# Graph layer with sorted edges: narrower chunks of edges and another interleaving in the token loop

## The chip, the cores and the metric

One NeuronCore of a Trainium2 chip runs the whole program. The time is the device time of one execution in microseconds (us). A profile records one execution, instruction by instruction. Engines: TensorE (PE, with its weight loads as PEld), VectorE (DVE), ScalarE (ACT), GpSimd (POOL) and SyncE (SP), which here mostly issues DMA transfers.

## The reference

The layer takes 1250 tokens (graph nodes) of 768 numbers and 20,000 edges, sorted by their destination. It adds a graph attention block (two attention layers) and a linear attention block to x, and then a mixture of experts:

```python
src = jax.random.randint(..., (20000,), 0, 1250); dst = jax.random.randint(..., (20000,), 0, 1250)
_o = jnp.argsort(dst, stable=True); src = src[_o]; dst = dst[_o]
def gat_conv(x, src, dst, W, a_src, a_dst, bias, H, C, n):
    h = (x @ W).reshape(n, H, C)
    ...
    e = leaky_relu(s_src[src] + s_dst[dst]); emax = segment_max(e, dst)
    ee = exp(e - emax[dst]); alpha = ee / segment_sum(ee, dst)[dst]
    return segment_sum(alpha * h[src], dst) + bias
xn = _layernorm(x)
x = x + gnn(xn, edges) + linear_attention(xn)
x = x + experts(_layernorm(x))
```

The edges go through both attention layers only as sums over (source, destination) pairs, so it is enough to know how many edges each pair has.

## The kernel before

The tokens are ten tiles of 125 rows. The attention works on a dense table cntT of edge counts: 125 partitions (the low part lo of the source) by ten source tiles by 1250 destinations, plus the table absent that marks pairs without an edge. The function gps_block has these stages: set-up of weights (until about 55 us), the token loop (59 to 210 us), keys and values, queries, the two attention layers, the router, and from about 940 us the blocks of the experts. The change is in the set-up and the token loop.

**Counting.** The 20,000 sorted edges are 160 chunks (ECH) of 125 edges, one edge per partition. An edge has a key = destination x 10 + source tile, and rel = key - base, where base belongs to its chunk: ten times the first destination that the chunk is taken to reach. For each chunk, DVE compares the steps 0, 1, 2, ... with rel (line 377, tile wide, 500 columns of 16 bit, 1 where the edge's key is). For eight chunks at a time, DVE compares the steps with lo (line 374, tile los). PE multiplies the two (line 387): the product adds the chunk's edges to counts in PSUM (pc), 125 by 500 for a block of 50 destinations (CB). A chunk reaches at most two blocks, so it gives one or two products, each only over its columns. There are six buffers of wide, whose second half is zeros, written once by POOL (line 345); the zeros are read where a product opens a block and has to write all of its 500 columns.

When the last chunk of a block is in, the function counted has ACT copy the counts to cntT (line 348). When a tile of 125 destinations is complete, the function there adds the loops of nodes on themselves (DVE, line 356), has ACT copy the tile to 16 bits (358), PE transpose it in two groups of five (ptc, 362) and DVE compare each group with zero (absent, 363).

**Edges outside.** The kernel takes sorted edges to lie near their expected place: chunk c reaches from destination (c // 16) x 125 + (c % 16) x 8 - 22 over CW = 50 destinations. Lines 328 to 336 count the edges outside of this (off, offs, a product po, off_i). After the token loop all engines read off_i (line 424), and where it isn't zero, a branch (425) counts everything again with full masks.

**Token loop.** For each tile, DVE normalises (401), POOL adds the bias (402), PE transposes in two groups of three (pt, 406), ACT copies to xnT (407), and PE makes two times six products with the graph weights (ph, 411, 400 columns in 32 bit), whose sums DVE scales into G (415). The chunks are a generator, parts, from which the loop takes one chunk after an even product k and two after an odd one (nine for six products).

**Order.** A planner places each instruction on its engine's queue with estimated times and priorities, so an engine's order is near that of the code and not the same; each engine then works its queue in order. 11 of the 120 token products are placed behind the branch.

Of the kernel before, what the change touches and what calls it, by code (L numbers as in the profile page):

```python
# [1 line left out]

# [6 lines left out]
F32 = mybir.dt.float32  # L9
F16 = mybir.dt.float16  # L10
# [5 lines left out]
ALU = mybir.AluOpType  # L16
# [3 lines left out]
P = 128  # L20
TP = 125
NT = 10
N = TP * NT
# [10 lines left out]
NPAIR = NH // 2  # L34
NE, HID, HS = 8, 768, 384
ECH = 160
CB, CW = 50, 50
HT = NT

# [9 lines left out]
CG = CO + 2  # L51

TINY = 2.0 ** -64


def part_bcast(ap, parts, n):
# [5 lines left out]
def gps_block(ctx: ExitStack, tc: tile.TileContext, x, src, dst, norm_g, norm_b, W1, a_src1, a_dst1, b1,  # L62
              W2, a_src2, a_dst2, b2, Wu, bu, w_qkv, w_proj, b_proj, router_w, w_gate, w_up, w_down,
              ws_gate, ws_up, ws_down, sg_w, sg_b, out):
    nc = tc.nc
# [33 lines left out]
    edp = edpool.enter_context(tc.tile_pool(name="edges", bufs=1, side="right", reuse_waits="tile"))  # L99
    wg = edp.tile([P, KD, H1 * CG], F32, name="wg")  # L100

    steps16 = edp.tile([TP, 2 * CB * HT], F16, name="steps16")
    nc.gpsimd.iota(steps16, pattern=[[1, 2 * CB * HT]], base=0, channel_multiplier=0,
                   allow_small_or_imprecise_dtypes=True)
# [6 lines left out]
    lo16 = edp.tile([TP, ECH], F16, name="lo16")  # L111
    key = edp.tile([TP, ECH], F32, name="key")
    rel = edp.tile([TP, ECH], F32, name="rel")
    bw = edp.tile([TP, 2, 2 * CG], F32, name="bw")
    bias = edp.tile([TP, 2, HALF], F32, name="bias")

# [44 lines left out]
    with tc.tile_pool(name="ph1", bufs=1, reuse_waits="tile") as p1, tc.tile_pool(name="ph1w", bufs=2, reuse_waits="tile") as p1w, \  # L161
# [55 lines left out]
        for j in range(2):  # L217
            o = H2 * (C2 + 1) + j * H2
# [11 lines left out]
        for k in range(KD):  # L230
# [10 lines left out]
            for h in range(H1):  # L241
                o = (h % 2) * CG
                for i in range(2):
                    nc.tensor.matmul(pm[:, h // 2, o:o + CG], wt[:, 2 * h + i, :], w2x[:, 2 * h + i, :],
                                     start=(i == 0), stop=(i == 1))
# [5 lines left out]
        for h in range(H1):  # L251
            o = (h % 2) * CG
# [9 lines left out]
        for s in range(2):  # L262
            half = slice(s * HALF, (s + 1) * HALF)
            nc.tensor.matmul(pb2[:, s, :HALF], ones[:2, :], br[:, half], start=True, stop=False)
            for h in range(H2):
                nc.tensor.matmul(pb2[:, s, :HALF], bc[:, 24 + h:25 + h].to_broadcast([C2, TP]), wub[:, h, half], start=False,
                                 stop=(h == H2 - 1))
# [5 lines left out]
        for h in range(H2):  # L273
            o = h * (C2 + 1) + C2
# [16 lines left out]
        nc.vector.tensor_scalar(hi, src_f, float(TP), None, op0=ALU.is_ge)  # L291
        for m in range(2, HT):
            nc.vector.scalar_tensor_tensor(hi, src_f, float(m * TP), hi, op0=ALU.is_ge, op1=ALU.add)
        nc.vector.scalar_tensor_tensor(lo, hi, -float(TP), src_f, op0=ALU.mult, op1=ALU.add)
        nc.vector.tensor_copy(lo16, lo)
        nc.vector.scalar_tensor_tensor(key, dst_f, float(HT), hi, op0=ALU.mult, op1=ALU.add)

        base = p1.tile([TP, ECH], F32, name="base")
        nc.gpsimd.iota(base, pattern=[[TP * HT, ECH // 16], [8 * HT, 16]], base=-22 * HT, channel_multiplier=0,
                       allow_small_or_imprecise_dtypes=True)  # L300
        nc.vector.tensor_sub(rel, key, base)

    def weights(dst_tile, w):
# [14 lines left out]
    with tc.tile_pool(name="cnt", bufs=1, reuse_waits="tile") as cp, \  # L318
# [7 lines left out]

        off = cp.tile([TP, ECH], F32, name="off")
        nc.vector.tensor_scalar(off, rel, 0.0, None, op0=ALU.is_lt)
        nc.vector.scalar_tensor_tensor(off, rel, float(CW * HT), off, op0=ALU.is_ge, op1=ALU.add)
        offs = cp.tile([TP, 2], F32, name="offs")  # L330
        nc.vector.tensor_reduce(offs[:, 0:1], off, axis=AX.X, op=ALU.add)
        nc.vector.memset(offs[:, 1:2], 1.0)
        po = ps.tile([P, 4, P], F32, name="po", tag="tr")
        nc.tensor.matmul(po[0:1, 0, 0:1], offs[:, 0:1], offs[:, 1:2], start=True, stop=True)
        off_i = cp.tile([1, 1], I32, name="off_i")
        nc.vector.tensor_copy(off_i, po[0:1, 0, 0:1])

        NB = N // CB
        BC = CB * HT
        firsts = [c // 16 * TP + c % 16 * 8 - 22 for c in range(ECH)]  # L340
        reach = [range(max(f, 0) // CB, (min(f + CW, N) - 1) // CB + 1) for f in firsts]

        wide = [cp.tile([TP, 2 * BC], F16, name=f"wide{i}") for i in range(6)]
        for w in wide:
            nc.gpsimd.memset(w[:, BC:], 0.0)

# [21 lines left out]
        def chunks():  # L368
            LB = 8
            open_ = {}  # L370
            for c in range(ECH):
                if c % LB == 0:
                    los = cp.tile([TP, LB, TP], F16, name="los", bufs=2)
                    nc.vector.tensor_tensor(los, lo16[:, c:c + LB, None].to_broadcast([TP, LB, TP]),
                                            steps16[:, None, :TP].to_broadcast([TP, LB, TP]), ALU.is_equal)
                w = wide[c % 6]
                nc.vector.tensor_scalar(w[:, :BC], steps16[:, :BC], rel[:, c:c + 1], None, op0=ALU.is_equal)
                for b in reach[c]:
                    new = b not in open_
                    if new:  # L380
                        open_[b] = pcp.tile([TP, 512], F32, name="pc")

                    o = (b * CB - firsts[c]) * HT
                    a = max(-o, 0)
                    e = BC if new else min(BC, BC - o)
                    last = c == ECH - 1 or b not in reach[c + 1]
                    nc.tensor.matmul(open_[b][:, a:e], los[:, c % LB, :], w[:, o + a:o + e], start=new, stop=last)
                    if last:
                        counted(b, open_.pop(b))
                yield  # L390

        parts = chunks()
        for t0 in range(0, NT, 2):
            ts = range(t0, t0 + 2)
            mv, r, r2 = ahead
            if t0 + 2 < NT:
                ahead = norm(t0 + 2)
            for i, t in enumerate(ts):
                tok = slice(t * TP, (t + 1) * TP)
                xn = p1w_.tile([TP, D], F32, name="xn")  # L400
                nc.vector.tensor_scalar(xn, acc[:, t, :], mv[:, i, 0:1], r[:, i:i + 1], op0=ALU.subtract, op1=ALU.mult)
                nc.gpsimd.tensor_add(acc[:, t, :], acc[:, t, :], bias.rearrange("p s d -> p (s d)"))
                for k0 in range(0, KD, 3):
                    pt = ps.tile([P, 4, P], F32, name="pt", tag="tr")
                    for k in range(3):
                        nc.tensor.transpose(pt[:, k, :TP], xn[:, (k0 + k) * P:(k0 + k + 1) * P], ident[:TP, :TP])
                    nc.scalar.copy(xnT[:, k0:k0 + 3, tok], pt[:, 0:3, :TP])
                for s in range(2):
                    ph = ps.tile([TP, 512], F32, name="ph", tag="mm", bufs=3)
                    for k in range(KD):  # L410
                        nc.tensor.matmul(ph[:, :2 * CG], xnT[:, k, tok], wg[:, k, s * 2 * CG:(s + 1) * 2 * CG],  # L411
                                         start=(k == 0), stop=(k == KD - 1))
                        for _ in range(1 + k % 2):
                            next(parts, None)
                    nc.vector.scalar_tensor_tensor(G[:, t, 2 * s:2 * s + 2].rearrange("p h c -> p (h c)"),
                                                   ph[:, :2 * CG], r2[:, i:i + 1], bw[:, s], op0=ALU.mult, op1=ALU.add)
                nc.gpsimd.tensor_copy(s1[:, t].rearrange("p j h -> p h j"), G[:, t, :, CO:CG])
                nc.gpsimd.memset(G[:, t, :, CO:CO + 1], 1.0)
# [6 lines left out]
        with tc.If(n_off > 0):  # L425
            for b0 in range(0, NB, 2):
# [3 lines left out]
                for c in range(ECH):  # L430
                    nc.vector.tensor_scalar(lof[c % 2], steps16[:, :TP], lo[:, c:c + 1], None, op0=ALU.is_equal)
                    nc.vector.tensor_scalar(wide[c % 2], steps16, relg[:, c:c + 1], None, op0=ALU.is_equal)
                    for i, pc in enumerate(pcs):
                        nc.tensor.matmul(pc[:, :BC], lof[c % 2], wide[c % 2][:, i * BC:(i + 1) * BC],
                                         start=(c == 0), stop=(c == ECH - 1))
# [26 lines left out]
    class Largest:  # L462


        def __init__(self, name, ss, sd, H):
            self.name, self.ss, self.sd, self.H = name, ss, sd, H
            self.srow = rows(ss, H, f"{name}_srow", TINY)
            self.mx = p3.tile([TP, NT, H], F32, name=f"{name}_mx")
# [15 lines left out]
        def columns(self):  # L484

            name, H, ss, sd = self.name, self.H, self.ss, self.sd
            z = p3.tile([TP, NT, H], F32, name=f"{name}_z")
            nc.vector.scalar_tensor_tensor(z, self.mx, 1.0 / TINY, sd, op0=ALU.mult, op1=ALU.add)
            em = p3.tile([TP, NT, H], F32, name=f"{name}_em")
# [9 lines left out]
    with tc.tile_pool(name="ph2", bufs=1, reuse_waits="tile") as p2:  # L499
# [14 lines left out]
        with tc.tile_pool(name="kvw", bufs=2, side="right", reuse_waits="tile") as p2w, tc.tile_pool(name="kvps", bufs=2, space=PSUM, reuse_waits="tile") as ps:  # L514
# [5 lines left out]
            for pr in range(0, NPAIR, 2):  # L520

                wkv = wkv0
                if pr > 0:
                    wkv = (p2w if pr == 2 else early).tile([P, KD, 2, 2 * P], F32, name=f"wkv{pr}", bufs=1,
                                                           tag="wkv" if pr == 2 else "early")
# [81 lines left out]
    with tc.tile_pool(name="h2p", bufs=1, reuse_waits="tile") as hp, tc.tile_pool(name="gatw", bufs=2, reuse_waits="tile") as pw:  # L607
# [87 lines left out]
        with tc.tile_pool(name="wup", bufs=1, side="right", reuse_waits="tile") as wp2, \  # L695
# [55 lines left out]
            o = H2 * (C2 + 1)  # L751
# [54 lines left out]
    with tc.tile_pool(name="fln", bufs=2, reuse_waits="tile") as pw, tc.tile_pool(name="flnps", bufs=2, space=PSUM, reuse_waits="tile") as ps:  # L806
# [4 lines left out]
                                base=0, pattern=[[1, TP]], channel_multiplier=-1)  # L811
        steps = pw.tile([TP, NE, -(-N // PART)], F32, name="steps", bufs=1)
        nc.gpsimd.iota(steps, pattern=[[0, NE], [PART, -(-N // PART)]], base=0, channel_multiplier=0,
                       allow_small_or_imprecise_dtypes=True)
        jb = pw.tile([TP, NBLK * NPART, NE], F32, name="jb", bufs=1)
        nc.gpsimd.iota(jb, pattern=[[1, NBLK * NPART], [0, NE]], base=0, channel_multiplier=0,
                       allow_small_or_imprecise_dtypes=True)
        odd = pw.tile([TP, -(-NBLK // 2), 2], F32, name="odd", bufs=1)
        nc.gpsimd.iota(odd, pattern=[[0, -(-NBLK // 2)], [1, 2]], base=0, channel_multiplier=0,
                       allow_small_or_imprecise_dtypes=True)  # L820
# [4 lines left out]
                       allow_small_or_imprecise_dtypes=True)  # L825
        rev = pw.tile([TP, NT, NE], F32, name="rev", bufs=1)
        nc.gpsimd.iota(rev, pattern=[[0, NT], [-1, NE]], base=NE, channel_multiplier=0,
                       allow_small_or_imprecise_dtypes=True)
# [18 lines left out]
        for r in range(2):  # L847
            m = pw.tile([TP, NT], F32, name=f"r_m{r}", bufs=1)
            nc.vector.tensor_reduce(m, pb, axis=AX.X, op=ALU.max)
            o = pw.tile(S3, F32, name=f"r_o{r}", bufs=1)  # L850
            nc.vector.tensor_tensor(o, pb, m[:, :, None].to_broadcast(S3), ALU.is_equal)
            nc.vector.tensor_mul(o, o, rev)
            f = pw.tile([TP, NT], F32, name=f"r_f{r}", bufs=1)
# [10 lines left out]
        pc = ps.tile([P, 512], F32, name="pc", tag="m")[:TP, :2 * NT * NE].rearrange("p (i t e) -> p i t e", i=2, e=NE)  # L864
# [14 lines left out]
        for e in range(NE):  # L879
# [3 lines left out]
                                       op0=ALU.mult, op1=ALU.add)  # L883
# [16 lines left out]
        for r in range(2):  # L900
# [7 lines left out]
            for t in range(NT):  # L908
                nc.tensor.matmul(pids[:, r * NBLK:(r + 1) * NBLK], spot[:, t, :], numb[:, t, :], start=(t == 0),
                                 stop=(t == NT - 1))  # L910
# [38 lines left out]
        for c0, cw in CHUNKS:  # L949
            for f in range(nh):  # L950
                pg = sps.tile([P, 512], F32, name="pg")
                pu = sps.tile([P, 512], F32, name="pu3")
                for pt, i in ((pg, 0), (pu, 1)):
                    for k in range(KD):
                        nc.tensor.matmul(pt[:, :cw], wsg[i][:, k, f * P:(f + 1) * P], xnT[:, k, c0:c0 + cw],
                                         start=(k == 0), stop=(k == KD - 1))
# [152 lines left out]
    with tc.tile_pool(name="comb", bufs=1, reuse_waits="tile") as cb, tc.tile_pool(name="cps", bufs=3, space=PSUM, reuse_waits="tile") as ps:  # L1109
# [12 lines left out]
        for t in range(2, NT):  # L1122
# [6 lines left out]
            for u in range(2 * (t - 3), min(2 * (t - 3) + 2, NT)):  # L1129
                for r in range(2):  # L1130
                    nc.vector.scalar_tensor_tensor(acc[:, u, :], ygs[u][:TP, r, :], g2[:, u, r:r + 1], acc[:, u, :],  # L1131
                                                   op0=ALU.mult, op1=ALU.add)
# [31 lines left out]
```

## Time and profile before

| | |
|---|---|
| median of 3 runs | 1597.15 us (1594.57 to 1598.87) |
| the profiled execution | 1597.16 us, span 1595.1 us |
| PE busy | 1525.0 us, 96% |
| DVE busy | 724.4 us, 45% |
| ACT busy | 367.6 us, 23% |
| POOL busy | 98.1 us, 6% |
| first and last chunk product | 59.6 and 190.9 us |

The span is from the first to the last instruction in the profile. Busy shares are averages over stages; in the token loop DVE is far busier than its 45%. A row of instructions gives line, engine, operation, output <- input, shapes and count, then the busy time in us and the mean duration of one in ns, then the engine's idle time right before these instructions and who ended it. A row of waits gives who waited for whom, the total in us, the number of waits and the longest. Durations of PE products include the time until the results are out, during which the next product already runs; the time from start to start is shorter.

### The profile page before, as it was taken

How to read it: one execution, taken by the hardware profiler on the slowest of the kernel's cores; microseconds unless marked ns; L12 is line 12 of the kernel's file. 1: busy time of each engine (PE TensorE's matmuls, PEld its weight loads, DVE VectorE, ACT ScalarE, POOL GpSimd, SP SyncE). 2: the span in 40 equal slices, each digit the busy share in tenths (PEclk: the TensorE clock that was granted, in tenths of full speed). 3: DMA queues.
4: the chain of work that ended last, by engine and by line, in shares of the span. 5: the costliest groups of instructions: out<-in, count | busy, mean ns of one | idle time of the engine just before them, and what ended most of it. 6: DMA issues, size and time to landing. Idle time of an engine off the chain costs nothing. (4 is left out here: it accounts for less than half of the span.)

```text
span 1595.1 us, 18670 instructions
## 1 busy us (share of the span) xinstructions
PE 1525.0 (96%) x7143; PEld 855.7 (54%) x7143; DVE 724.4 (45%) x1355; ACT 367.6 (23%) x630; POOL 98.1 (6%) x144
## 2 busy tenths in 40 slices
PE   5999889999999989999999999999999999999986
PEld 5666544444454669896555554444444444444443
DVE  7889639411535359996799651111111111111116
ACT  3222211111101048881276310101111010111100
POOL 2211000000000000000000100000100001000000
PEclk9999989999999999999999999999999999999998
DMA  7100031001201111002121343688888888888727
GB/s 202 40 1 1 2 132 65 7 0 50 63 10 50 40 46 33 33 17 78 33 62 49 108 176 151 218 316 321 301 311 317 317 308 307 307 326 312 265 101 270
DMA packets 92835, 229.18 MB, mean 144 GB/s; under 512 B 5431, under 2 KB 28061, under 8 KB 92742
## 3 DMA queue, kind: packets, MB, share of 16 engines
q1 hardware_dynamic: 84428, 199.30, 35.8%
q0 software_dynamic: 6112, 27.95, 5.0%
q8 instruction: 64, 1.05, 0.3%
q10 hardware_dynamic: 2202, 0.64, 0.2%
q14 instruction: 29, 0.24, 0.0%
HBM read 212.42 MB, written 16.43 MB: 143 GB/s over the span
## 5 line engine op out<-in xcount | busy, mean ns | idle before, releaser
L1012 PE MATMUL pgb<-wg,xT 128*64 128x384 f32 (+1 forms) x1056 | 178.8, 488 | 0.5 <-ACT xT L1019 0.5
L1012 PE MATMUL pdb<-wd,hT 128*64 128x384 f32 (+1 forms) x1056 | 175.1, 488 | 1.4 <-SPq L1092 1.4
L1012 PE MATMUL pub<-wu,xT 128*64 128x384 f32 (+1 forms) x1056 | 174.0, 486 | 0.0
L533 PE MATMUL pp<-wkv,xnT 128*125 128x512 f32 x360 | 160.8, 595 | 0.1
L615 PE MATMUL pa<-G,u 125*125 125x199 f32 x800 | 140.4, 336 | 11.2 <-DVE h L623 6.0
L615 PEld LDWEIGHTS pa<-G,u 125*125 125x125 f32 x800 | 135.6, 189 | 16.2 <-issue 7.2
L1012 PEld LDWEIGHTS pub<-wu,xT 128*64 128x64 f32 x1056 | 75.7, 137 | 94.5 <-issue 94.5
L1012 PEld LDWEIGHTS pdb<-wd,hT 128*64 128x64 f32 x1056 | 74.6, 137 | 91.6 <-issue 87.0
L1012 PEld LDWEIGHTS pgb<-wg,xT 128*64 128x64 f32 x1056 | 73.7, 137 | 90.7 <-issue 89.8
L533 PEld LDWEIGHTS pp<-wkv,xnT 128*125 128x125 f32 x360 | 65.6, 189 | 73.1 <-issue 72.7
L1031 DVE TENSOR_TENSOR h<-h,pgb 128x384 f32<-128x384 f32 x44 | 24.4, 554 | 171.7 <-ACT h L1030 171.7
L1042 DVE COPY y<-pdb 128x768 f32<-128x768 f32 x22 | 21.1, 958 | 178.8 <-PE pdb L1012 178.8
L411 PE MATMUL ph<-wg,xnT 128*125 128x400 f32 x240 | 99.6, 521 | 2.5 <-PEq L425 2.4
L598 DVE SCALAR_TENSOR_TENSOR u<-ea,cntT 125x625 f32<-125x625 f32 x120 | 93.9, 805 | 12.6 <-PE pa L615 8.0
L595 ACT ACTIVATE eb<-r,g_ss 125x625 f32<-125x625 f32 x120 | 95.0, 816 | 20.3 <-DVE ea L596 20.3
L596 DVE TENSOR_TENSOR ea<-ea,eb 125x625 f32<-125x625 f32 x120 | 94.0, 805 | 8.2 <-ACT ea L593 5.4
L480 DVE CUSTOM_DVE_ANT_0 junk<-ssb,absent 125x1250 bf16<-125x1250 f32 x60 | 87.8, 1463 | 11.7 <-DMA ssb<-g_srow_d 10.4
L1030 ACT ACTIVATE h<-pgb 128x384 f32<-128x384 f32 x44 | 21.6, 491 | 307.6 <-PE pgb L1012 307.6
L563 PE MATMUL pq<-xnT,wq 128*128 128x500 f32 (+1 forms) x216 | 82.6, 527 | 4.6 <-DMA wq<-in_L_mix_w_qkv_dram 4.5
L1036 DVE TENSOR_TENSOR h<-h,pub 128x384 f32<-128x384 f32 x44 | 24.4, 554 | 134.4 <-PE pub L1012 134.4
L715 PE MATMUL pu<-wu,xnT 128*125 128x384 f32 x240 | 82.1, 487 | 1.3 <-DVE acc L720 1.3
L576 PE MATMUL pu<-wp,at 128*125 128x384 f32 x240 | 80.4, 488 | 1.0 <-DVE acc L579 1.0
(267 smaller groups left out, 1666.9 us busy)
## 6 DMA issues: line engine op xcount, KB each, us to landing
wg<-in_L_ffn_w_gate_dram SPq DMA_DIRECT2D x22, 2304.0 KB, 8.4
wu<-in_L_ffn_w_up_dram SPq DMA_DIRECT2D x22, 2304.0 KB, 10.4
wd<-in_L_ffn_w_down_dram SPq DMA_DIRECT2D x22, 2304.0 KB, 9.6
yg<-ys SPq DMA_DIRECT2D x10, 768.0 KB, 9.4
r<-g_rrow_d SPq DMA_DIRECT2D x12, 625.0 KB, 4.0
wq<-in_L_mix_w_qkv_dram SPq DMA_DIRECT2D x18, 384.0 KB, 3.5
wkv<-in_L_mix_w_qkv_dram SPq DMA_DIRECT2D x6, 768.0 KB, 12.3
acc<-in_x_dram POOLq DMA_DIRECT2D x10, 375.0 KB, 10.6
```

The costliest lines, as they stand in the source:

```text
L411: nc.tensor.matmul(ph[:, :2 * CG], xnT[:, k, tok], wg[:, k, s * 2 * CG:(s + 1) * 2 * CG], start=(k == 0), stop=(k == KD - 1))
L480: nc.vector.tensor_tensor_reduce(out=junk, in0=self.ssb[:TP], in1=absent[:, dt, :], scale=1.0, scalar=-3.0e38, op0=ALU.add, op1=ALU.max, a ...
L533: nc.tensor.matmul(pp, xnT[:, k, tok], wkv[:, k, :, :], start=(k == 0), stop=(k == KD - 1))
L563: nc.tensor.matmul(pq[:, :qw], wq[:, k, :], xnT[:, k, tok], start=(k == 0), stop=(k == KD - 1))
L576: nc.tensor.matmul(pu[:, s, :HALF], at[:, k, i * TP:(i + 1) * TP], wp[:, k, s * HALF:(s + 1) * HALF], start=(k == 0), stop=(k == KD - 1))
L595: nc.scalar.activation(eb, r[:TP, 1, :], AF.Exp, bias=ss02[:, st, h:h + 1])
L596: nc.vector.tensor_max(ea, ea, eb)
L598: nc.vector.scalar_tensor_tensor(u, ea, 1.0, cntT[:, st, half * W:(half + 1) * W], op0=ALU.min, op1=ALU.mult)
L615: nc.tensor.matmul(pa[i][:, :CO + 1], u[:, i * TP:(i + 1) * TP], G[:, st, h, :CO + 1], start=(st == 0), stop=(st == NT - 1))
L715: nc.tensor.matmul(pu[:, :HALF], xnT[:, k, t * TP:(t + 1) * TP], wus[s][:, k, :], start=(k == 0), stop=(k == KD - 1))
L1012: nc.tensor.matmul(pt[part, :HALF], rows[:, k, part], w[:, k, s * HALF:(s + 1) * HALF], start=(k == 0), stop=(k == KD - 1))
L1031: nc.vector.tensor_mul(h, h, pgs[s][:, :HALF])
```

## The change

The reach of a chunk follows its place. The 160 chunks are 20 spans (SPANS) of eight (SPAN). Sorted random destinations stray most in the middle and little at the ends, so each span has its own margin STRAY (9 nodes at the ends to 20 in the middle) and WIDTH = 2 x STRAY + 9 (27 to 49 nodes). The function first_of gives a chunk's first destination. A mask is then WIDTH x 10 columns wide (270 to 490) where no block is opened, else 500 as before.

base is now filled span by span, with a new tile reached that holds the width (20 iotas and 20 memsets on POOL in place of one iota). The check for edges outside compares with reached (one DVE instruction more), its product goes to the PSUM pool of the counts, and off_i is copied by ACT. wide has eight buffers. In the token loop four chunks are taken after product 2 and five after product 5 of each six.

```diff
-CB, CW = 50, 50
+CB = 50
+SPAN = 8
+SPANS = ECH // SPAN
+STRAY = [math.ceil(40 * ((n := min(g + 1, SPANS - g)) * (SPANS - n)) ** 0.5 / SPANS) for g in range(SPANS)]
+WIDTH = [2 * m + 9 for m in STRAY]
...
+def first_of(c):
+    g, i = divmod(c, SPAN)
+    return g * N // SPANS + i * 8 - STRAY[g]
...
+    reached = edp.tile([TP, ECH], F32, name="reached")
...
-        nc.gpsimd.iota(base, pattern=[[TP * HT, ECH // 16], [8 * HT, 16]], base=-22 * HT, channel_multiplier=0,
-                       allow_small_or_imprecise_dtypes=True)
+        for g in range(SPANS):
+            cols = slice(g * SPAN, (g + 1) * SPAN)
+            nc.gpsimd.iota(base[:, cols], pattern=[[8 * HT, SPAN]], base=first_of(g * SPAN) * HT, channel_multiplier=0,
+                           allow_small_or_imprecise_dtypes=True)
+            nc.gpsimd.memset(reached[:, cols], float(WIDTH[g] * HT))
...
-        nc.vector.scalar_tensor_tensor(off, rel, float(CW * HT), off, op0=ALU.is_ge, op1=ALU.add)
+        far = cp.tile([TP, ECH], F32, name="far")
+        nc.vector.tensor_tensor(far, rel, reached, ALU.is_ge)
+        nc.vector.tensor_add(off, off, far)
...
-        po = ps.tile([P, 4, P], F32, name="po", tag="tr")
-        nc.tensor.matmul(po[0:1, 0, 0:1], offs[:, 0:1], offs[:, 1:2], start=True, stop=True)
+        po = pcp.tile([TP, 512], F32, name="pc")
+        nc.tensor.matmul(po[0:1, 0:1], offs[:, 0:1], offs[:, 1:2], start=True, stop=True)
         off_i = cp.tile([1, 1], I32, name="off_i")
-        nc.vector.tensor_copy(off_i, po[0:1, 0, 0:1])
+        nc.scalar.copy(off_i, po[0:1, 0:1])
...
-        firsts = [c // 16 * TP + c % 16 * 8 - 22 for c in range(ECH)]
-        reach = [range(max(f, 0) // CB, (min(f + CW, N) - 1) // CB + 1) for f in firsts]
-        wide = [cp.tile([TP, 2 * BC], F16, name=f"wide{i}") for i in range(6)]
+        firsts = [first_of(c) for c in range(ECH)]
+        cols = [WIDTH[c // SPAN] * HT for c in range(ECH)]
+        reach = [range(max(f, 0) // CB, (min(f + w // HT, N) - 1) // CB + 1) for f, w in zip(firsts, cols)]
+        wide = [cp.tile([TP, 2 * BC], F16, name=f"wide{i}") for i in range(8)]
...
-                w = wide[c % 6]
-                nc.vector.tensor_scalar(w[:, :BC], steps16[:, :BC], rel[:, c:c + 1], None, op0=ALU.is_equal)
+                w = wide[c % len(wide)]
+                n = cols[c] if all(b in open_ for b in reach[c]) else BC
+                nc.vector.tensor_scalar(w[:, :n], steps16[:, :n], rel[:, c:c + 1], None, op0=ALU.is_equal)
...
-                    e = BC if new else min(BC, BC - o)
+                    e = BC if new else min(BC, cols[c] - o)
...
-                        for _ in range(1 + k % 2):
+                        for _ in range({2: 4, 5: 5}.get(k, 0)):
                             next(parts, None)
```

## The prediction

> **What bounds the kernel now.** I read the busy digits first, then the same engines over the stretch that the change touches, then what waited there, then single instructions. The page:
>
> ```profile
> PE   5999889999999989999999999999999999999986
> DVE  7889639411535359996799651111111111111116
> ACT  3222211111101048881276310101111010111100
> PEclk9999989999999999999999999999999999999998
> ```
>
> One digit is 39.9 us. TensorE (PE) is at 9 nearly everywhere. The token loop lies in digits 2 to 5; there VectorE (DVE) shows 8 too, so the stage needs both engines looked at. Busy time by stretch (clock third from the right; the counts in brackets are instructions):
>
> ```profile
> 60.00:194.90 134.90, 129.02 (x677) 82.70 (x676) 110.53 (x278) 35.57 (x60) 18.29 (x26) 1.00 0.01 3
> 194.90:205.10 10.20, 7.77 (x15) 3.86 (x16) 0.57 (x1) 0.95 (x2) 0.00 (x0) 0.50 0.02 5
> ```
>
> In 134.9 us PE is busy for 129.0 (96%), DVE for 110.5 (82%). Then come 10.2 us at half clock. The waits of this stretch:
>
> ```profile
> ACT cntT L348 <- PE pc L387: 76.2, 22, 5.3
> DVE wide L377 <- PE pc L387: 12.2, 24, 1.0
> PE ptc L362 <- ACT c L358: 4.2, 4, 1.6
> PE ph L411 <- PEq L425: 2.4, 1, 2.4
> PE pt L406 <- DVE absent L363: 1.4, 4, 0.6
> ```
>
> DVE waits 12.2 us for PE to hand back mask buffers; PE waits for no mask at all. PE sets the pace, interrupted by short chains through ScalarE (ACT) and DVE. What one product costs:
>
> ```profile
> L387 PE MATMUL pc<-wide,los 125*125 125x500 f16 x30 | 11.3, 376 | 0.0
> L387 PE MATMUL pc<-wide,los 125*125 125x100 f16 x10 | 2.1, 206 | 0.0
> L411 PE MATMUL ph<-wg,xnT 128*125 128x400 f32 x240 | 99.6, 521 | 2.5 <-PEq L425 2.4
> L377 DVE TENSOR_SCALAR wide<-steps,rel 125x500 f16<-125x500 f16 x160 | 50.7, 355 | 12.6 <-PE pc L387 12.2
> ```
>
> A mean contains the pipeline's latency, which the next product overlaps; the price is the slope: (376 - 206) / 400 columns = 0.425 ns a column. A token product (120 in the code, 240 passes in the row) takes 2 x 335 ns from start to start in the trace. A mask of 500 columns takes 258 ns start to start on DVE.
>
> **The change, part by part.**
>
> *Fewer columns.* Counting the chunk products as the built programs list them: 309 with 90,370 columns before, 291 with 79,530 after. 10,840 x 0.425 ns = 4.6 us off PE. The stage has no slack on PE, so this is gained in full unless something else becomes late.
>
> *Fewer changes between the two kinds of product.* Ahead of the branch the built order has 109 token products in 85 stretches before, in 33 after. From start to start, the 83 stretches of two or more passes have a first pass that takes 1.9 us in all beyond 335 ns each, and the chunk products right before a stretch 1.5 us in all beyond their columns: 3.4 us, 40 ns a stretch. 52 x 40 ns = 2.1 us; between 0.5 (were only the median of some 10 ns real) and 2.1. I take 2.0, as the mean is what adds up.
>
> *The chain chunk, count, transposes.* Each of ten transposed tiles (ptc) needs the last product of its counts, an ACT copy (0.58), a DVE addition (0.29), an ACT copy (1.24): 2.1 us. In the built order before, PE has 2.0 to 2.3 us of other work in between nine times and 0.7 us the last time; after, 2.1 to 2.8 nine times and none the last. That costs 0.7 us at the end of the stage. The 5-wide transposes pt that follow a ptc need its PSUM buffers back, two DVE instructions (absent) of 0.76 us. Before, two such places have little work between (0.84 and 0.63 us of chunk products), and the trace shows 0.5 and 0.9 us lost there. After, four have: 0.54, 0.64, 1.16 and 0.65 us of work, so by the same rows about 0.6, 0.9, 0.2 and 0.8 us. Loss 1.0 us. Last places of the stage:
>
> ```profile
> 193.41 0.79 PE L362 MATMUL ptc<-ident,c 125*125 125x125 f16 x10 [1.59 <-ACT c L358]
> 194.81 1.60 PE L406 MATMUL pt<-ident,xn 125*128 125x125 f32 x6 [0.61 <-DVE absent L363]
> 200.36 9.98 PE L411 MATMUL ph<-wg,xnT 128*125 128x400 f32 x22 [2.43 <-PEq L425]
> ```
>
> *Half clock there.* The Trainium skill ("TensorE: Matmul & The Clock Gate", "Part 1: The HAM clock gate") says that idling over a window of about 3.4 us halves the clock, and that windows run freely. The row: 194.9 to 205.1 at 0.50, three such windows, just after the idle places above, and none from 60 to 194.9. By the row alone the tail stays as it is, cost 0; by the rule the phase can shift it by a window either way, and 3.4 us at half clock costs 1.7 us. I take 0 and keep 1.7 both ways.
>
> *VectorE.* Mask columns fall from 80,000 to 70,250. 258 ns for 500 columns is, with four elements a cycle at 0.96 GHz (an estimate by the first page below), 0.26 ns a column over a fixed 128; 9,750 x 0.26 = 2.5 us off DVE, hidden behind PE, gain 0. Here a rule speaks against the change: widths are (2m + 9) x 10, so half of 490 is 245, an odd number of 2-byte elements. "VectorE: DVE Perf Modes", section "Mode 2×_1P — pack two bf16 into one 32-bit read", asks for 4-byte alignment; "Vector Engine (DVE) Microarchitecture Reference", section "5.1 Performance modes — why throughput varies by op and dtype", measured that it makes no difference if the count is even. The row L377 has only 500, whose half is even. By the first, 57,750 columns in 135 masks cost 0.52 instead of 0.26 ns: DVE up 12.5 us against before; by the second, down 2.5. I take the second, as it is a measurement of this shape, and keep the first as a rival. Group by group, with DVE at most eight chunks ahead, DVE falls behind once, by 0.8 us (chunks 31 to 42, where PE has no token product); a ptc wait lies there anyway. Cost 0, at most 0.8.
>
> *The check for stray edges.* One DVE instruction more (0.24 us, L329's kind, start to start) ahead of the first chunk. In it, off_i moves to ACT: DVE loses a wait of 3.32 us on the product po, and ACT gets a copy of some 0.2 us (as short as its 125x2 ones) between b1w and the xnT copies; PE has four chunk products (0.55 us) before it needs xnT. PE is busy until 59.1 us with L271, so nothing of this shows; without that cover it would be 0.2 to 0.5 us. po's place in another PSUM pool frees a transpose buffer: nothing waits for it.
>
> *GpSimd (POOL).* One iota becomes 20 iotas and 20 memsets, plus two memsets of 0.51 us for the new mask buffers:
>
> ```profile
> 23.70 0.32 POOL L299 IOTA base<- 125x160 f32 x1
> 32.41 0.73 POOL L322 MEMSET rest<- 3x768 f32 x1 [8.38 <-PE p_w L235]
> 40.45 0.97 POOL L345 MEMSET wide<- 125x500 f16 x2 [6.39 <-DVE bw L239]
> ```
>
> 40 instructions at 0.16 (L418's memset) to 0.32 us are 6.4 to 12.8 us, ending at 30 to 36.5. Queued behind are rest, whose store SP issues at 33.2 and which would be up to 4 us late, and the mask memsets, which idle 6.4 us until 40.45 anyway. SP's next load behind it waits until 54.65 for other work. rel needs base at 51.3. Cost 0; were POOL four times slower, 51.3 would be missed.
>
> Sum: -4.6 - 2.0 + 0.7 + 1.0 = -4.9 us. What follows the loop keeps its length and starts earlier. The profiled execution took 1597.16 us (span 1595.1, 2.1 around it), the median of the runs is 1597.15: the sum needs no scaling. **1592.2 us.**
>
> **The rivals.**
>
> *B, more than the sum:* a mask lead of eight chunks in place of six gets the DVE addition out earlier, and the three ptc waits of about 0.9 us beyond the usual 0.2 vanish (2.2 us), and a half-clock window goes at the end (1.7): 1588.3. For it: DVE did wait 12.2 us for buffers. Against it: two additions stand right behind a 1.19 us los instruction in the new order too.
>
> *C, the gain is given back on PE:* idle time at ptc and pt now falls together. The trace has 1.2 us of idling around 105 us without loss of clock and 1.6 us at the end with it; three of the four new places have up to 1.9 us. Two windows at half clock cost 3.4: 1595.6.
>
> *D, slower, VectorE becomes the bound:* half-rate masks. DVE's 110.5 us become 123.0; its own waits on others (24.4 idle less the 12.2 for buffers) add 12.2: 135.2, as long as the 134.9 of before. Half of the 9 us that PE waits fall outside of it, and 0.7 at the end: +5.3, 1602.5. It decides once a mask of 490 columns takes about 0.36 us start to start; at 0.26 it is gone. Against it: the measured page.
>
> *E, the change doesn't do what it says:* an edge outside its chunk's reach would send the kernel through the branch that counts all again. The reference's edges stay five nodes inside the low end and nine inside the high end of every chunk's reach. Excluded.
>
> **How the numbers follow.** As summed 0.54: its centre lies at the bound of 0.3% (4.8 us, about what a measurement of this kernel can tell), spread 2 us, leaning to the faster side by the switches that could hide more: 0.33 faster, 0.21 within. B 0.17, faster. C 0.09, within. D 0.20, slower. Faster 0.50, same 0.30, slower 0.20. The likeliest case alone spans 1589 to 1595. The range: half of D is above 1602.5, and a twentieth to a tenth, B's far end, below 1586.5.
>
> **What would show it.** Column slope unchanged and 291 chunk products: the 4.6. The last chunk product at about 185 instead of 190.9 us. Mask rows of 490 columns near 355 ns mean (A) or near 480 (D); a PE wait on DVE's masks, absent now, would mean D. Digits below 10 in the clock between 60 and 185 us: C. POOL's last reached later than 51 us, or DVE idle before rel, would undo the POOL step. It goes wrong if the waits at ptc grow from their 4.2 us by more than 2.

## The result, and the profile after

| | before | after |
|---|---|---|
| median | 1596.26 us (1594.47 to 1598.87, 7 runs) | 1590.88 us (1585.89 to 1593.91, 7 runs) |
| ratio, 95% interval | | 0.9956 [0.9939, 0.9974] |
| the profiled execution | 1597.16 us, span 1595.1 | 1587.15 us, span 1585.4 |
| mean granted clock of PE | 0.985 | 0.992 |
| first and last chunk product | 59.62 and 190.87 us | 56.58 and 184.73 us |
| next stage (keys and values) starts | 211.07 us | 204.02 us |

The kernel became faster by 0.44% [0.26, 0.61], 7.0 us by that ratio and 5.4 us between the medians of all runs. The profiled pair differs by 10.0 us, more than either, and its page has to be read with that in mind: 3.0 us lie ahead of the first chunk product, 4.0 us between it and the next stage (151.45 against 147.44), and some 2.6 us behind that, in stages that the change leaves alone.

The busy digits of the profile after:

```profile
PE   5999889998999989999999999999999999999996
DVE  7888559311726359896799551111111111111116
ACT  3222211111101058881376310101111010111100
PEclk9999999999999999999999999999999999999998
```

PE is as full as before. Its busy time by stretch, with the clock third from the right, first the token loop up to its last chunk, then the end of the stage:

```profile
60.00:187.00 127.00, 120.10 (x633) 78.08 (x632) 100.53 (x270) 34.52 (x58) 17.80 (x26) 1.00 0.00 1
187.00:200.00 13.00, 8.38 (x31) 4.75 (x32) 2.16 (x3) 1.11 (x3) 0.00 (x0) 0.87 0.02 5
```

PE works 95% of the loop and DVE 79%, so PE still sets the pace. The clock is full throughout the loop. At the end it is halved for 3.4 us here; a second profile of the same kernel (a0_after below) has 10.2 us of it, as before had. The waits in the loop:

```profile
ACT cntT L369 <- PE pc L409: 68.9, 21, 5.9
PE ptc L383 <- ACT c L379: 5.6, 4, 2.3
DVE wide L399 <- PE pc L409: 5.1, 7, 1.6
PE ph L433 <- PEq L448: 3.6, 1, 3.6
PE pt L428 <- DVE absent L384: 1.6, 7, 0.6
PE pc L409 <- DVE wide L399: 0.6, 1, 0.6
```

DVE waits 5.1 us for mask buffers in place of 12.2. PE waits at ptc for 5.6 us (4.2 before), at pt for 1.6 (1.4), and now once for a mask, 0.6. The groups, with busy time and mean ns of one:

```profile
L433 PE MATMUL ph<-wg,xnT 128*125 128x400 f32 x240 | 89.0, 511 | 3.7 <-PEq L448 3.6
L409 PE MATMUL pc<-wide,los 125*125 125x500 f16 x25 | 9.4, 376 | 0.0
L409 PE MATMUL pc<-wide,los 125*125 125x270 f16 x12 | 3.0, 278 | 0.0
L399 DVE TENSOR_SCALAR wide<-steps,rel 125x490 f16<-125x490 f16 x54 | 16.4, 344 | 0.9 <-PE pc L409 0.9
```

A column still costs (376 - 278) / 230 = 0.426 ns. A mask of 490 columns has a mean of 344 ns, no more than one of 500 had (355). Last, the end of the stage in order of time:

```profile
187.22 0.79 PE L383 MATMUL ptc<-ident,c 125*125 125x125 f16 x10 [2.26 <-ACT c L379]
...
188.62 0.54 PE L428 MATMUL pt<-ident,xn 125*128 125x125 f32 x3 [0.61 <-DVE absent L384]
...
194.27 9.02 PE L433 MATMUL ph<-wg,xnT 128*125 128x400 f32 x22 [3.61 <-PEq L448]
```

The last count tile makes PE wait 2.26 us, 0.67 more than the 1.59 of before.

These rows agree with what the prediction said of a column, of a mask and of the last wait. Two things they leave open. The 4.0 us between the first chunk product and the next stage are less than the 4.9 forecast for the loop, although this end of the stage has less half clock; in a0_after, with the same 10.2 us of it as before, that stretch takes 148.83 us, 2.6 less than the 151.45 of before. And the prediction doesn't explain the 3.0 us ahead of the first chunk product.

### The profile page after: what moved, and what is told of

The parts are those of the page before. It is cut to its first block, busy times and chain, and to the rows that moved or that the text cites. A ratio compares the mean times of both kernels' runs of the same rounds, so it can differ in the third digit from the quotient of the medians.

```text
span 1585.4 us, 18641 instructions
## 1 busy us (share of the span) xinstructions
PE 1512.6 (95%) x7125; PEld 849.4 (54%) x7125; DVE 720.0 (45%) x1355; ACT 367.6 (23%) x631; POOL 99.0 (6%) x185
## 5 line engine op out<-in xcount | busy, mean ns | idle before, releaser
L503 DVE CUSTOM_DVE_ANT_0 junk<-ssb,absent 125x1250 bf16<-125x1250 f32 x60 | 87.8, 1463 | 12.2 <-DMA ssb<-g_srow_d 10.9
L433 PE MATMUL ph<-wg,xnT 128*125 128x400 f32 x240 | 89.0, 511 | 3.7 <-PEq L448 3.6
```

The source lines that it names most:

```text
L503: nc.vector.tensor_tensor_reduce(out=junk, in0=self.ssb[:TP], in1=absent[:, dt, :], scale=1.0, scalar=-3.0e38, op0=ALU.add, op1=ALU.max, a ...
```

## The experiments

Ratios are against runs of the kernel before on the same chip, beside those of the experiment; a gain or loss in us below is the ratio times the median of before. "First pc" is the first chunk product, "next stage" the first product pp of the keys and values, both of the profiled execution.

| | median us | ratio | first pc | next stage |
|---|---|---|---|---|
| n0_before | 1596.82 | 1.0000 [0.9992, 1.0009] | 56.6 | 211.0 |
| e1_reach | 1591.70 | 0.9968 [0.9956, 0.9979] | 55.8 | 206.4 |
| e2_interleave | 1597.89 | 1.0002 [0.9993, 1.0011] | 55.6 | 214.0 |
| e3_six | 1591.38 | 0.9968 [0.9955, 0.9980] | 56.9 | 206.1 |
| a0_after | 1590.97 | 0.9965 [0.9951, 0.9978] | 55.7 | 204.5 |
| e4_old_po | 1593.28 | 0.9977 [0.9967, 0.9987] | 54.8 | 208.1 |
| e5_full_masks | 1590.40 | 0.9958 [0.9945, 0.9971] | 56.4 | 206.6 |
| e6_ten | 1591.80 | 0.9968 [0.9956, 0.9980] | 60.3 | 205.3 |
| e7_po_only | 1591.89 | 0.9979 [0.9971, 0.9987] | 55.8 | 206.3 |
| e8_reach_po | 1589.01 | 0.9961 [0.9949, 0.9974] | 56.7 | 202.9 |
| e9_pool_dve | 1590.26 | 0.9962 [0.9950, 0.9974] | 56.7 | 204.3 |
| e10_no_bias | 1585.49 | 0.9934 [0.9921, 0.9947] | 56.3 | 200.1 |

### The kernel before and the kernel after once more (n0_before, a0_after)

No edit in either.

> The kernel before once more. Theory 1 (the half clock in the set-up at 51.5 us and the length of the tail's half clock are a matter of the windows' phase): within 0.3% of before, and its profile may have the set-up's half-clock window or not. Theory 2 (the half clock in the set-up belongs to the order of before, and the change removed it): the window at about 51 us is there again, and the first chunk product comes at 59 to 60 us.

> The changed kernel once more, as the yardstick of this group. Theory 1 (the phase of the clock windows): the set-up's half clock may be there or not, and the first chunk product comes at 56.5 or 59.5 us. Theory 2 (the change removed it): never there, 56.5 us.

Both times repeat. The new profile of the kernel before is what opened the case: its first chunk product comes at 56.64 us, 3.0 us earlier than in the profile that the prediction had, and yet its last one comes at 190.62, as late as there (190.87). Something eats the 3.0 us. The timeline of n0_before about the first transposes (start, us, engine, line, idle before and its releaser):

```profile
54.14 4.21 DVE L377 TENSOR_SCALAR wide<-steps,rel 125x500 f16<-125x500 f16 x4
...
54.45 3.75 POOL L402 TENSOR_TENSOR acc<-acc,bias 125x768 f32<-125x768 f32 x2 [8.23 <-ACT bias L268]
...
56.27 0.54 PE L406 MATMUL pt<-ident,xn 125*128 125x125 f32 x3
...
59.38 0.14 DVE L336 CAST off_i<-po 1x1 int32<-1x1 f32 x1
...
59.58 0.54 PE L406 MATMUL pt<-ident,xn 125*128 125x125 f32 x3 [2.52 <-DVE off_i L336]
```

The transposes of a tile come in two groups of three, each in a buffer of the PSUM pool of tag "tr", which has two. The first group takes one, po holds the other, and the second group has to wait until DVE has read po into off_i. DVE's copy stands behind four masks, which take 4.21 us here, just while POOL does two bias additions, and behind an instruction of line 374. PE waits 2.52 us for a number that nobody needs before the branch.

In the profile that the prediction had, the same place looks different. The timeline of the kernel before there:

```profile
55.73 3.46 PE L271 MATMUL pb<-w2x,bc 96*125 96x198 f32 x12
...
59.13 0.19 PE L334 MATMUL po<-offs 125*1 125x1 f32 x2
...
59.25 0.54 PE L406 MATMUL pt<-ident,xn 125*128 125x125 f32 x3
...
59.35 0.14 DVE L336 CAST off_i<-po 1x1 int32<-1x1 f32 x1 [3.32 <-PE po L334]
...
59.87 0.48 PE L406 MATMUL pt<-ident,xn 125*128 125x125 f32 x3
```

There PE had half clock from 51.5 to 58.3 us (0.62 on average from 51 to 60), so L271 lasted until 59.1 and the product po came only then; DVE, done with its masks, waited for PE. The second group of transposes starts at 59.87 in one case and at 59.58 in the other: either PE is slow or it waits. This half clock doesn't belong to the order of before (theory 2): n0_before hasn't got it, and e6_ten, which has the change, has it from 51.6 to 58.5 us, with its first chunk product at 60.3.

### Only the narrow reach (e1_reach)

From the kernel after, everything but the reach taken back:

```diff
-        po = pcp.tile([TP, 512], F32, name="pc")
-        nc.tensor.matmul(po[0:1, 0:1], offs[:, 0:1], offs[:, 1:2], start=True, stop=True)
+        po = ps.tile([P, 4, P], F32, name="po", tag="tr")
+        nc.tensor.matmul(po[0:1, 0, 0:1], offs[:, 0:1], offs[:, 1:2], start=True, stop=True)
...
-        nc.scalar.copy(off_i, po[0:1, 0:1])
+        nc.vector.tensor_copy(off_i, po[0:1, 0, 0:1])
...
-        wide = [cp.tile([TP, 2 * BC], F16, name=f"wide{i}") for i in range(8)]
+        wide = [cp.tile([TP, 2 * BC], F16, name=f"wide{i}") for i in range(6)]
...
-                        for _ in range({2: 4, 5: 5}.get(k, 0)):
+                        for _ in range(1 + k % 2):
```

> Only the narrower reach: one or two chunks after each product and six mask buffers as before, off_i on VectorE. Theory of the columns: 10,840 columns at 0.425 ns off TensorE, 4 to 5 us faster than before (ratio 0.9970 to 0.9975), with 84 stretches of token products. Rival (the interleaving carries the gain): within 1.5 us of before.

0.9968 [0.9956, 0.9979], 5.1 us: the columns alone are worth what the prediction had for them, 4.6 us. The wait for off_i is in its trace too, 2.54 us, so it isn't part of this gain.

### Only the interleaving (e2_interleave)

From the kernel before:

```diff
-                        for _ in range(1 + k % 2):
+                        for _ in range({2: 4, 5: 5}.get(k, 0)):
```

> Only the interleaving: four and five chunks after products 2 and 5, all else as before. Theory of the columns: 49 changes of product fewer save 1 us by the trace of the changed kernel (and 2 by the prediction), the waits at the transposes take as much: within 1.5 us of before. Rival (the interleaving carries the gain): 3 us or more faster.

1.0002 [0.9993, 1.0011]: nothing. The 35 stretches of token products left in its trace lose 2.8 us at the switches, where the 83 of before lost 3.4. Its waits show where that goes:

```profile
PE ptc L362 <- ACT c L358: 5.1, 4, 2.3
...
PE pt L406 <- DVE off_i L336: 2.6, 1, 2.6
PE pt L406 <- DVE absent L363: 2.5, 7, 0.6
```

ptc has 0.9 us more than before and the transposes behind absent 1.1 more. That is more than the switches gave. The wait for off_i stands here as well.

### The kernel after with one part changed (e3_six, e4_old_po, e5_full_masks, e6_ten)

```diff
e3_six:
-        wide = [cp.tile([TP, 2 * BC], F16, name=f"wide{i}") for i in range(8)]
+        wide = [cp.tile([TP, 2 * BC], F16, name=f"wide{i}") for i in range(6)]
e4_old_po: po and off_i as in e1_reach, all else as after
e5_full_masks:
-                n = cols[c] if all(b in open_ for b in reach[c]) else BC
+                n = BC
e6_ten:
-                        for _ in range({2: 4, 5: 5}.get(k, 0)):
+                        for _ in range({2: 5, 5: 5}.get(k, 0)):
```

> The changed kernel with six mask buffers in place of eight. Prediction's main case (buffers are no cause): within 1 us of the changed kernel. Rival B (the longer lead of the masks matters): 2 us or more slower than the changed kernel, and more waits of TensorE at the transposes of counts.

0.9968 against 0.9965 and 0.9956 of the kernel after. With six buffers PE waits at ptc 6.4 us in five places and behind absent 2.4, with eight 5.6 in four and 1.6: the lead of eight is worth 1.6 us in the trace and nothing that the times can tell.

> The changed kernel with the check's product and off_i as before: the product in the transposes' PSUM pool, its copy on VectorE. Prediction (no cost either way, TensorE is busy there): within 0.5 us of the changed kernel; VectorE waits about 3 us for the product before the first masks. Rival: the early masks matter, 2 us or more slower than the changed kernel.

0.9977, 1.9 us behind a0_after, with intervals that overlap. Its waits have the line again that n0_before has:

```profile
PE pt L428 <- DVE off_i L356: 2.7, 1, 2.7
```

> The changed kernel with all masks 500 columns wide, the products as narrow as in the changed kernel. VectorE has 2.5 us more work. Prediction (VectorE is hidden): within 0.5 us of the changed kernel. Rival (VectorE sets part of the pace): 2 us or more slower. If odd halves cost half the rate, it would be faster and the 490-column masks of the changed kernel would take some 125 ns longer than 500-column ones.

0.9958: writing all 500 columns of each mask costs nothing. DVE is busy for 106.56 us between 57 and 185 us in place of the 102.65 of a0_after, and it has room for that: PE waits 1.0 us for masks in place of 0.6. The groups of its masks:

```profile
L399 DVE TENSOR_SCALAR wide<-steps,rel 125x500 f16<-125x500 f16 x160 | 53.2, 381 | 4.7 <-PE pc L409 4.7
```

> The changed kernel with five and five chunks after products 2 and 5, so that the chunks run out one product group earlier and 13 token products stand between the last transposes and the branch. Theory of the end chain: the 2.4 us wait at the last transposes stays partly, the idling of the end spreads, 0 to 2 us faster than the changed kernel. Rival (the number per group only moves work about): within 0.5 us.

0.9968: ten chunks in place of nine for six token products change nothing that the times can tell.

### Only the place of po and off_i (e7_po_only)

From the kernel before:

```diff
-        po = ps.tile([P, 4, P], F32, name="po", tag="tr")
-        nc.tensor.matmul(po[0:1, 0, 0:1], offs[:, 0:1], offs[:, 1:2], start=True, stop=True)
+        po = pcp.tile([TP, 512], F32, name="pc")
+        nc.tensor.matmul(po[0:1, 0:1], offs[:, 0:1], offs[:, 1:2], start=True, stop=True)
...
-        nc.vector.tensor_copy(off_i, po[0:1, 0, 0:1])
+        nc.scalar.copy(off_i, po[0:1, 0:1])
```

> The kernel before with one edit: the check's product in the PSUM pool of the counts, its copy off_i on ScalarE. New theory (the second group of transposes waits 2.5 us for the transpose buffer that po holds until VectorE has copied off_i, unless TensorE happens to come later): that wait is gone from the trace, 1.5 to 3 us faster than before, the token products start at 57 us whenever the set-up runs at full clock. The prediction's step (the move of po gains nothing): within 0.5 us of before.

0.9979 [0.9971, 0.9987] over 22 runs: 3.4 us [2.1 to 4.6], of an edit that the prediction had at nothing. The timeline of e7_po_only:

```profile
55.02 0.19 PE L334 MATMUL pc<-offs 125*1 125x1 f32 x2 [0.41 <-ACT b1w L272]
55.14 0.86 PE L406 MATMUL pt<-ident,xn 125*128 125x125 f32 x6
...
56.39 2.18 PE L411 MATMUL ph<-wg,xnT 128*125 128x400 f32 x6
```

All six transposes follow each other and the token products begin at 56.39; in n0_before they began at 60.50. The losses in its loop are those of before (ptc 4.2 us, pt 1.6).

The 3.4 us are more than the wait of 2.5 us, and the clock seems to have a part in it. Four of the traces here have the wait, and in two of them half clock begins during the wait or right behind it: from 59.0 to 62.4 us in e4_old_po, and from 57.5 to 64.3 in e2_interleave, where the first six passes of token products take 4.18 us in place of the 2.18 above:

```profile
58.57 0.89 PE L406 MATMUL pt<-ident,xn 125*128 125x125 f32 x3 [2.58 <-DVE off_i L336]
...
60.31 4.18 PE L411 MATMUL ph<-wg,xnT 128*125 128x400 f32 x6
```

Over the whole execution, 13 of the 22 of e7_po_only had a mean granted clock of 0.991 or 0.992, which none of the 28 of before beside them had (0.985 to 0.990). The four at 0.987 took 1596.8 to 1597.3 us, no less than the seven of before at 0.987 (1595.3 to 1597.4). So the traces show that the wait is gone; how much of the 3.4 us is the wait and how much is clock, in this place or others, isn't measured.

### Is it the buffer or the engine? (e9_pool_dve)

The move has two parts: another PSUM pool, and ACT in place of DVE. This takes the second back, from the kernel after:

```diff
-        nc.scalar.copy(off_i, po[0:1, 0:1])
+        nc.vector.tensor_copy(off_i, po[0:1, 0:1])
```

> The changed kernel with only half of the move undone: po stays in the PSUM pool of the counts, off_i is copied by VectorE again. If the held buffer is the cause: no wait of the transposes for off_i, within 0.5 us of the changed kernel. Rival (VectorE's waiting for po delays its masks): 1.5 us or more slower than the changed kernel, as with both halves undone.

0.9962 [0.9950, 0.9974], as the kernel after. The timeline of e9_pool_dve:

```profile
55.96 0.86 PE L428 MATMUL pt<-ident,xn 125*128 125x125 f32 x6
...
59.02 0.14 DVE L356 CAST off_i<-pc 1x1 int32<-1x1 f32 x1
```

DVE copies off_i as late as in n0_before, and nobody waits for it. It was the held buffer, then; which engine copies makes no difference that the times can tell.

### Without the interleaving (e8_reach_po)

From the kernel after:

```diff
-                        for _ in range({2: 4, 5: 5}.get(k, 0)):
+                        for _ in range(1 + k % 2):
```

> The changed kernel with the old interleaving, one or two chunks after each product; reach, eight buffers and the move of po stay. If the interleaving by itself gains nothing: the reach (5.2 us) and po (2 to 3) add up, 1588.5 to 1590.5, no slower than the changed kernel. Rival (the interleaving helps once the reach is narrow, by its 51 fewer changes of product): 1 us or more slower than the changed kernel.

0.9961 [0.9949, 0.9974], 1589.01 us, no slower than the kernel after. In the trace it reaches the next stage at 202.9 us, the kernel after at 204.0 and 204.5. Counted from the first chunk product, it takes 146.2 us against 148.8 in a0_after, whose end has the same 10.2 us of half clock. With e2_interleave this says that the interleaving contributes nothing, and in the traces costs 1 to 3 us. This is the fastest kernel measured here that does all of the work, but the times can't tell it from the kernel after.

### Without POOL's bias additions (e10_no_bias)

From the kernel after, the ten additions of line 424 left out, and so the bias from the result:

```diff
-                nc.gpsimd.tensor_add(acc[:, t, :], acc[:, t, :], bias.rearrange("p s d -> p (s d)"))
```

> The changed kernel without GpSimd's ten additions of the bias in the token loop; this leaves the bias out of the result. Theory (each addition holds up VectorE's next instruction by about 1.4 us, and with it the chain to the transposes of counts): VectorE's 4.5 us for six masks at 53 us become 1.3, the waits of TensorE for the transposes' inputs fall by 2 us or more, and the time by 2 to 4 us. Rival (VectorE has slack for them): within 1 us of the changed kernel.

0.9934 [0.9921, 0.9947]: 4.5 to 4.9 us faster than e9_pool_dve and a0_after, whose intervals it doesn't touch, and more than the 2 to 4 expected, although no instruction of PE was removed. In the traces of both kernels PE, DVE and ACT work the same instructions in the same order through the whole loop, so it isn't a new order either. The masks of 270 columns in a0_after:

```profile
L399 DVE TENSOR_SCALAR wide<-steps,rel 125x270 f16<-125x270 f16 x14 | 6.5, 512 | 1.1 <-PE pc L409 1.1
```

and in e10_no_bias:

```profile
L399 DVE TENSOR_SCALAR wide<-steps,rel 125x270 f16<-125x270 f16 x14 | 3.3, 285 | 1.1 <-PE pc L409 1.1
```

Fourteen masks take little more than half as long once POOL doesn't add at the same time. Six of them in a row, ahead of the first chunk products, in the timeline of the kernel after, with the two additions that run meanwhile:

```profile
53.44 4.47 DVE L399 TENSOR_SCALAR wide<-steps,rel 125x270 f16<-125x270 f16 x6
...
53.58 3.57 POOL L424 TENSOR_TENSOR acc<-acc,bias 125x768 f32<-125x768 f32 x2 [7.24 <-ACT bias L283]
```

and in that of e10_no_bias:

```profile
53.19 1.34 DVE L399 TENSOR_SCALAR wide<-steps,rel 125x270 f16<-125x270 f16 x6
```

The difference is 3.13 us, in 3.57 us of POOL. The Trainium skill ("SBUF — State Buffer", section "Who interferes with whom") says that DVE in its two-port modes and GpSimd share a pair of ports, and that whoever comes second stands still until the other's instruction is through. The rows agree in size: with masks standing still for the whole of the additions it would be at most 3.57 us. The waits at ptc in e10_no_bias:

```profile
PE ptc L383 <- ACT c L379: 2.4, 2, 2.3
```

5.6 us have become 2.4, almost all of it the end of the stage. So of the four places where PE waits for the chain of the counts, two are gone and a third is down from 1.35 to 0.16 us: they were there because POOL held up a DVE instruction. The next stage starts 4.2 us earlier than in e9_pool_dve, with 3.4 us of half clock at the end in both. That is shown by removal only. Whether the additions can be put where they hold up nothing wasn't run, and stays open.

## Why the prediction was right, and where it was not

The forecast of 1592.2 us is 1.3 us from the median, a sum of -4.9 us against -5.4 between the medians and -7.0 by the ratio. Its steps, one by one:

**Fewer columns, -4.6.** Right. The price of a column is the same (0.426 ns), and the edit alone measured -5.1 us (e1_reach).

**Fewer changes of product, -2.0.** Half. From start to start the switches cost 3.40 us before (83 stretches) and 2.36 after (32 stretches): 1.0 gained. The step took the mean of 40 ns a stretch as a price, but each of the remaining stretches costs 74 ns. What makes up the rest of it stays open.

**The chain of counts, +0.7, and the transposes, +1.0.** The end is exact, 1.59 to 2.26 us. The other ptc waits grew by 0.7 us, which the step had at zero (nearly all of these waits went with POOL's additions in e10_no_bias), and the pt waits by 0.2 in place of 1.0. Together +1.6 us against +1.7. Chain and switches therefore come to about +0.6 for the interleaving where the prediction had -0.3; alone it measured +0.3 us [-1.1 to 1.8] (e2_interleave).

**Half clock, 0.** Right for the loop, where the clock is 1.00 from 60 to 187 us. At the end the two profiles of the kernel after have 3.4 and 10.2 us of it, so there the phase does decide, as the step allowed with its 1.7 us both ways.

**VectorE, 0.** Right. Masks of 490 columns take 258 ns from start to start, as those of 500 do (259), so the odd half costs nothing, and the page of the Trainium skill that the prediction followed ("Vector Engine (DVE) Microarchitecture Reference", section 5.1) holds for this shape. PE's one wait for a mask, at 84 us, is 0.6 us, within the 0.8 allowed. e5_full_masks shows that the columns saved on DVE are hidden.

**GpSimd, 0.** Right with room to spare. The last instruction on reached starts at 24.96 us, against 30 to 36.5 forecast, since a pair of iota and memset goes by in 0.13 us:

```profile
24.89 0.14 POOL L316 IOTA base<- 125x8 f32 x1
24.96 0.11 POOL L318 MEMSET reached<- 125x8 f32 x1
```

**po and off_i, 0.** This step failed. It read: "PE is busy until 59.1 us with L271, so nothing of this shows", and "po's place in another PSUM pool frees a transpose buffer: nothing waits for it". The move gained 3.4 us alone (e7_po_only) and 1.9 between e4_old_po and a0_after, and the second group of transposes is what waits, for 2.5 to 2.7 us. The cover that was named was PE at half clock, which two of the 14 executions profiled had at that place (before and e6_ten). The price that was put on losing the cover, 0.2 to 0.5 us, counted the copy on ACT but not the buffer that the copy on DVE had kept. DVE's idle time of 3.32 us at off_i was read as DVE waiting for PE; that is what it was, and with PE 3 us earlier it turns into PE waiting for DVE.

So the three parts measured alone come to -5.1 + 0.3 - 3.4 = -8.2 us, while the whole measured -7.0 [-9.7 to -4.1] and again, as a0_after, -5.6 [-7.8 to -3.5]. That the forecast came so close is in part luck: a step at zero was worth 2 to 3 us, and the loop, forecast at 4.9, gave less (4.0 and 2.6 in the two traces of the kernel after). Whether the parts hinder one another by 1 or 2 us, or this is the error of the three measurements, the runs don't settle; by the trace the interleaving would be the part that takes it.

**The rivals.** B (eight buffers do away with ptc waits) is out: they grew, and six buffers cost only 0.8 us of them. C (half clock in the loop) and D (masks at half rate) are out by the clock of 1.00 and the 344 ns. C's readings of idle time were off: the trace of before has 0.7 us about 105 us, and 2.2 at the end (1.59 and 0.61). Two of the ptc waits do vanish when POOL's additions go: DVE was late there, but not for want of mask buffers.

## What to carry to other kernels

An edit is hidden only as far as its cover is there in every execution: where the cover is an engine at reduced clock, cost the edit once more as if that stretch ran at full speed, and ask what then waits for what. A small result that sits in a PSUM buffer of a pool with two buffers, until a busy engine gets round to a 0.14 us copy, can hold up the pool's next user for as long as that copy stands in the queue (2.5 us here), so give it a buffer that nobody else is waiting for. When a DVE row has a mean well above that of the same shape elsewhere (512 against 285 ns here), look at what POOL runs in those moments.

## What the runs showed of the hardware that was not expected

- Two POOL additions of 125x768 (1.8 us each) stretch six DVE masks from 1.34 to 4.47 us. All ten, 18.0 us of POOL's time, cost the kernel 4 to 5 us although PE, which they never touch, is the bound.
- The half clock late in the set-up comes and goes between executions of one kernel (6.8 us of it from 51.5 us in the first profile of before, none there in the second), and so do 6.8 us of it at the end of the loop (3.4 and 10.2 us in two profiles of the kernel after). What PE gains at the start where it has the full clock was lost again in the kernel before at off_i: the last chunk product came at 190.87 and 190.62 us.
- Forty small POOL instructions whose rows say 0.11 to 0.15 us each took 2.67 us in all, from 22.41 to 25.08, half the sum of their durations (5.16).
